# Quarter sums of a Strassen-style transformer block taken on VectorE from PSUM, first keys from eight products, and earlier reloads

## The chip, the core and the metric

The kernel runs on one core of a Trainium2 chip. Five engines work side by side, each with its own in-order instruction stream: TensorE (PE: matmuls, and transposes as matmuls against an identity; PEld is its weight load), VectorE (DVE), ScalarE (ACT), GpSimd (POOL) and SyncE (SP, which here only issues DMAs). They meet through semaphores. SBUF is the working memory, PSUM the memory into which PE writes. The metric is the device time of one execution in microseconds (us). Lower is better.

## The reference

A cross-attention block with an MLP, all in float32: 8 sequences of 256 tokens, width 512, 16 heads of 32, 256 context tokens for each sequence, an MLP of width 2048.

```python
x = layer_norm(hidden_states, ln1_w, ln1_b)
q = x @ q_w + q_b
k = encoder_hidden_states @ k_w + k_b
v = encoder_hidden_states @ v_w + v_b
attn = softmax(where(mask, q k^T / sqrt(32), min))      # per head
hidden = (attn @ v) @ cproj_w + cproj_b + hidden_states
y = layer_norm(hidden, ln2_w, ln2_b)
return hidden + gelu(y @ fc_w + fc_b) @ proj_w + proj_b
```

## The kernel before

**Groups and units.** The 8 sequences are worked as 4 groups of two (512 tokens). Each group has 8 units, one for each of 4 head groups (4 heads, 128 features) and each of the two sequences. `units` lists them; the loop at line 748 walks them. In the turn of unit n, PE makes the scores of unit n+2 (`scores`, L458), DVE takes them from PSUM with the mask and the running minimum (`softmax`, L476), ACT takes the exponential (L486), GpSimd multiplies by the reciprocal sums (`divide`, L500), PE turns the probabilities of unit n (`turn_probs`, L513, evicted in turn by DVE L516 and ACT L518), and PE multiplies them with the values (`attend`, L529; DVE L536 adds the value bias into the attention tile).

**Seven products in place of eight.** Each projection (keys `kT`, queries `qT`, values `v`, output `po`) is cut into quarters, "11", "12", "21", "22", and done by a Strassen scheme of Winograd's form with 7 products of four matmuls (`strassen`, pieces p0 to p6). It needs sums of quarters beforehand: `A_SUMS` of a weight (s2, s3, s4 and a changed "21"), `B_SUMS` of the token operand (t1, t2, t4 and a changed "12"). Each is one `tensor_tensor` of 128x512 by `sum_up`, L167, on the engine named in the call. For token operands, `sums_at` gives the first two to DVE and the last two to GpSimd; the value and output weights are summed on GpSimd, those of keys and queries on DVE. A piece's result leaves PSUM by `made`: on ACT (L374, L393), on DVE with an earlier sum added (L378, L395), or, for the output projection, on GpSimd and DVE together (L437, L438), into a residual tile.

**Through DRAM.** Finished quarters of keys, queries and values are staged in SBUF, stored to DRAM by `store_quarter`, and reloaded by head group (`load_qk`, `load_v`), two buffers to each. All of these go through SP's one queue in program order, as do loads of context (`load_ctx`), tokens (`load_x`), residual (`load_res`), weights, and stores of the hidden state. The eight bias and scale vectors are loaded on GpSimd's queue (L119).

**The order is written out by hand.** Nothing is scheduled by a planner (`manual_schedule`). Two tables say what is slipped into a unit's turn: `between[g, u, i]` (PE pieces, two places) and `aside[g, u, i]` (other work, four places, 3 being the unit's end). `share` deals projection pieces over units by the counts in `ns`; `begin` and `spread` put other work at a place (group, unit, position). While group g attends, group g+1's keys, queries and values are projected, and from group 1 on also an output projection of an earlier group. Group 3 has no next group: it carries the output projections of groups 1 and 2, the MLP's norm of group 0 and the sums of the fc weights. Everything before the loop (from line 694) is the prologue: group 0's three projections and the first two units' softmax.

**PSUM.** Four score banks, two projection banks (`ps_m`), and two banks under the tag `pt`, which turned contexts, turned tokens, turned probabilities and attention results share.

**Attention operand.** `Att` wraps the attention tile of a group with three sum tiles, made by `begin_out`; `sums_at(..., att_in, ...)` sums it later. Group 1's attention is spilled to DRAM and reloaded (`spill_att`, `reload_att`).

**MLP.** From line 807: four groups, each with four rounds of fc (7 products, L848 to L863 the evictions: u1 on ACT; u2, u3, h22, h12, h21 on DVE) and a projection. In group 0, `sum_pw` sums the projection weights on DVE (L805) in each round, and two rounds also sum the fourth block of fc weights; blocks 0 to 2 are summed in group 3 of the attention.

Of the kernel before, what the change touches and what calls it, by code (L numbers as in the profile page):

```python
# [22 lines left out]
def tile_xattn_block(  # L23
# [94 lines left out]
    for vec, n in vecs:  # L118
        nc.gpsimd.dma_start(rows[at : at + n, :], vec.rearrange("(n p) -> n p", p=P))  # L119
        col_of.append(at)  # L120
        at += n
# [121 lines left out]
    with ExitStack() as att:  # L243
# [6 lines left out]
        mbias, ctxT, xnT, vs, qk, probs, stats, att_of, res = ({} for _ in range(9))  # L250
# [17 lines left out]
        def turn_ctx(g):  # L268
            def piece(c):
                if c == 0:  # L270
                    ctxT[g] = tokens_operand(both, "cT", f"ctxT_{g}")
                ps = turned(f"pct_{g}_{c}")
                turn(ps, ctxs[g], c)
                nc.scalar.copy(chunk(ctxT[g], c), halves(ps))

            return [lambda c=c: piece(c) for c in range(NC)]
# [88 lines left out]
        def project_qk(g, tag):  # L365
            w, base = ("k", c_kb) if tag == "kT" else ("q", c_qb)

            def made(n, bank, u):
                o, k = int(n[0]) - 1, int(n[1]) - 1
                st = staged(g, tag, n)  # L370
                for i in range(2):
                    b = col(base, 2 * o + i)
                    if u is None:
                        nc.scalar.activation(  # L374
                            st[:, i, :], bank[:, i, :], AF.Identity, bias=b, scale=1.0
                        )
                    else:
                        nc.vector.scalar_tensor_tensor(  # L378
                            st[:, i, :], bank[:, i, :], b, u[:, i, :], ALU.add, ALU.add
                        )  # L380
                store_quarter(g, tag, o, k, st)

            return strassen(
                f"p{tag}_{g}", lambda: ws[w], lambda: (ctxT if tag == "kT" else xnT)[g], False, made
            )
# [27 lines left out]
        class Att:  # L413


            def __init__(self, g):
                self.t = att_of[g]
                self.sums = work.tile([P, 3, HC, S], F32, tag="as", bufs=1, name=f"as_{g}")
# [102 lines left out]
        def attend(n):  # L521

            g, hg, b = units[n]
            if hg == 0 and b == 0:
                att_of[g] = work.tile([P, NHG, G], F32, tag="att", name=f"att_{g}")
            av = ps_t.tile([P, S], F32, tag="pt", name=f"av_{n}")
            for kc in range(NK):
# [8 lines left out]
            nc.vector.tensor_scalar_add(  # L536
                att_of[g][:, hg, ts(b, S)], av, col(c_vb, hg)
            )
# [33 lines left out]
        def begin_out(g):  # L572
            att_in[g] = Att(g)

        def spill_att(g):
            nc.sync.dma_start(att_dram, att_of[g])
# [14 lines left out]
        def sums_at(place_v, place_g, of_, g, which):  # L591

            begin(*place_v, lambda: sum_up(V, of_[g], B_SUMS, *which[:2]))
            begin(*place_g, lambda: sum_up(GP, of_[g], B_SUMS, *which[2:]))
# [14 lines left out]
        for g in range(NG - 1):  # L609

            work_of = [project_qk(g + 1, "kT"), project_qk(g + 1, "qT"), project_v(g + 1)]
            ns = (1, 2), (1, 2), (1, 1), (1, 2), (1, 2), (1, 2), (1, 1), (1, 1)
            if g == 1:
                work_of.insert(2, project_out(0))
                ns = (2, 2), (1, 2), (1, 2), (2, 2), (2, 2), (1, 2), (2, 2), (1, 2)
# [4 lines left out]
            if g + 2 < NG:  # L620
                between[g, 7, 1] += turn_ctx(g + 2)
                sums_at((g, 7, 3), (g, 7, 3), ctxT, g + 2, ALL)
                begin(g, 1, 3, load_ctx, g + 2)
                begin(g, 3, 3, load_x, g + 2)
                norm_over(
                    g, xs, g + 2, "a", [(5, 1), (5, 2), (6, 1), (6, 2), (6, 3), (7, 1), (7, 1), (7, 2), (7, 2)]
                )
            sums_at((g, 1, 2), (g, 1, 3), xnT, g + 1, ALL)
            begin(g, 0, 3, load_mask, g + 1)
            begin(g, 5, 1, make_mask, g + 1)  # L630
            begin(g, 0, 3, load_qk, g, 2)
            begin(g, 2, 3, load_qk, g, 3)
            begin(g, 5, 3, load_qk, g + 1, 0)
            begin(g, 6, 3, load_qk, g + 1, 1)
            for hg in range(1, NHG):
                begin(g, 2 * hg - 2, 3, load_v, g, hg)
            begin(g, 7, 3, load_v, g + 1, 0)
        g = 1
        begin(g, 0, 0, begin_out, 0)
        sums_at((g, 0, 1), (g, 0, 1), att_in, 0, ALL)  # L640
        begin(g, 0, 3, load_res, 0)
        bias_at(0, g, [(1, 1), (1, 2), (2, 1), (2, 2)])
# [3 lines left out]
        sums_at((g, 7, 1), (g, 7, 1), att_in, 1, ALL)  # L646
        begin(g, 6, 3, load_res, 1)
        bias_at(1, g, [(7, 2), (7, 2), (7, 3), (7, 3)])
        g = NG - 1
        begin(g, 0, 3, load_qk, g, 2)  # L650
        begin(g, 2, 3, load_qk, g, 3)
        for hg in range(1, NHG):
            begin(g, 2 * hg - 2, 3, load_v, g, hg)
        share(g, project_out(1), [(0, 0, 1), (0, 1, 2), (1, 0, 1), (1, 1, 1), (2, 0, 1), (2, 1, 1)])
        share(g, project_out(2), [(3, 0, 1), (3, 1, 1), (4, 0, 1), (4, 1, 1), (5, 0, 1), (5, 1, 1), (6, 0, 1)])
        begin(g, 2, 3, begin_out, 2)
        sums_at((g, 2, 3), (g, 2, 3), att_in, 2, ALL)
# [4 lines left out]
        begin(g, 6, 3, begin_out, 3)  # L662
        begin(g, 7, 1, lambda: sum_up(V, att_in[3], B_SUMS, 0))
# [18 lines left out]
        for q in range(3):  # L682
            begin(g, 0, 3, load_fc, q)
        spread(
            g,
            [(u, i) for u in range(2, 8) for i in (1, 2)],
            [lambda q=q, i=i: sum_fc(q, i) for q in range(3) for i in range(4)],
        )
# [4 lines left out]

        load_ctx(0)
# [4 lines left out]
        load_mask(0)  # L699
# [3 lines left out]
        run(turn_ctx(0))  # L703
        ps = turned("ps_cols")
        nc.tensor.transpose(ps[:, :n_rows], rows, ident[:n_rows, :n_rows])
        nc.vector.tensor_copy(cols, ps[:, :n_rows])
        load_ctx(1)
        ws["c"] = weight("cw", cproj_w)
        sum_up(V, ctxT[0], B_SUMS, 0, 1)
        sum_up(GP, ctxT[0], B_SUMS, 2, 3)  # L710
        sum_up(V, ws["k"], A_SUMS, 0, 1, 2, 3)
        seen, roots, normalise = layer_norm(xs[0], "a0")
        run([*seen, roots, *normalise])
        k, q, v, tx = project_qk(0, "kT"), project_qk(0, "qT"), project_v(0), turn_x(0)
        run(k[:4])
        run(tx)
        load_x(1)
        sum_up(V, xnT[0], B_SUMS, 0, 1)
        sum_up(GP, xnT[0], B_SUMS, 2, 3)
        sum_up(V, ws["q"], A_SUMS, 0, 1, 2, 3)  # L720
        run(k[4:])
        make_mask(0)
        run(q)
        sum_up(GP, ws["v"], A_SUMS, 0, 1, 2, 3)
        load_qk(0, 0)
        run(v[:2])
# [3 lines left out]
        run(v[2:4])  # L730
        divide(0)
        seen, roots, normalise = layer_norm(xs[1], "a1")
        run([*seen[:2]])
        load_qk(0, 1)
        run(v[4:5])
# [3 lines left out]
        run(v[5:])  # L739
        divide(1)  # L740
        run([*seen[2:], roots, *normalise])
        load_v(0, 0)
        run(turn_ctx(1))
        sum_up(V, ctxT[1], B_SUMS, 0, 1)
        sum_up(GP, ctxT[1], B_SUMS, 2, 3)
        sum_up(GP, ws["c"], A_SUMS, 0, 1, 2, 3)
# [27 lines left out]
        sum_up(V, att_in[3], B_SUMS, 1, 2, 3)  # L774
        sum_up(GP, ys[0], B_SUMS, 0, 1, 2, 3)
        run(o)
# [3 lines left out]
    with ExitStack() as mlp:  # L780
# [26 lines left out]
        for g in range(NG):  # L807
# [21 lines left out]
            for q in range(HF // 2):  # L829
# [16 lines left out]

                fc(bank[1], "11", "11", q, True, False)
                nc.scalar.copy(u1, bank[1])  # L848
# [11 lines left out]
                nc.vector.tensor_tensor(h["12"][q], bank[7], u2, ALU.add)  # L860
                gelu("12", 1, h["12"][q])
# [6 lines left out]
                if g == 0:  # L868
                    sum_pw(q)
                    if q < 2:  # L870
                        sum_fc(3, 2 * q, 2 * q + 1)
# [121 lines left out]
```

## Time and profile before

| what | us |
|---|---|
| median of 3 runs (846.02 to 850.85) | 846.16 |
| the profiled execution | 843.05 |
| its span, first to last instruction | 841.3 |
| first scores on PE (L458) | 61.16 |
| first matmul of the MLP (L796) | 440.96 |
| last attend of group 0, 1, 2, 3 (start) | 165.96, 263.85, 342.18, 423.36 |
| busy on POOL in quarter sums (L167, eight rows of groups) | 47.4 |

The mean granted clock of TensorE is 0.970. The two halves read differently: up to 440 us the loop of units and projections, after it the MLP. A busy share is an average over both, so the times of single stretches say more. A wait in the profile is named by the engine that stood, its line, and what released it. Durations of a group of instructions are means unless a single start time is given.

### The profile page before, as it was taken

How to read it: one execution, taken by the hardware profiler on the slowest of the kernel's cores; microseconds unless marked ns; L12 is line 12 of the kernel's file. 1: busy time of each engine (PE TensorE's matmuls, PEld its weight loads, DVE VectorE, ACT ScalarE, POOL GpSimd, SP SyncE). 2: the span in 40 equal slices, each digit the busy share in tenths (PEclk: the TensorE clock that was granted, in tenths of full speed). 3: DMA queues.
4: the chain of work that ended last, by engine and by line, in shares of the span. 5: the costliest groups of instructions: out<-in, count | busy, mean ns of one | idle time of the engine just before them, and what ended most of it. 6: DMA issues, size and time to landing. Idle time of an engine off the chain costs nothing.

```text
span 841.3 us, 12003 instructions
## 1 busy us (share of the span) xinstructions
PE 768.5 (91%) x4417; PEld 636.9 (76%) x4417; DVE 420.1 (50%) x1035; ACT 270.7 (32%) x794; POOL 359.7 (43%) x311
## 2 busy tenths in 40 slices
PE   5687898899969998987689999999999999999997
PEld 4575776677757776865468888888888888888886
DVE  4636576676647675787564764222541234322100
ACT  2114664566436655644302310032101330023100
POOL 5504564277515543966572553132440425213430
PEclk9899899999979999998999999999999999999999
DMA  9422253234222423861129100120004000020001
GB/s 297 169 88 88 67 157 108 76 111 145 88 76 89 152 80 103 264 199 48 52 73 314 63 1 1 51 100 2 1 1 149 2 1 1 25 76 1 1 1 50
DMA packets 56554, 70.79 MB, mean 84 GB/s; under 512 B 3844, under 2 KB 37680, under 8 KB 56368
## 3 DMA queue, kind: packets, MB, share of 16 engines
q1 hardware_dynamic: 55824, 69.22, 24.9%
q0 software_dynamic: 672, 0.81, 0.6%
q8 instruction: 35, 0.57, 0.3%
q14 instruction: 23, 0.19, 0.1%
HBM read 47.99 MB, written 22.02 MB: 83 GB/s over the span
## 4 chain that ended last, share of the span: by engine, by line
PE 74%; DVE 8%; POOL 7%; DMA 5%; issue 3%; ACT 2%; SPq 1%; DVEq 0%; POOLq 0%
PE py L796 23%; PE pf L796 20%; PE ppt L513 6%; PE pqT L310 6%; PE pkT L310 5%; PE pv L310 4%; POOL pr L500 4%; PE s L458 4%; PE av L529 3%; PE po L310 2%; DMA qT<-qT_dram 2%; DMA pw<-in_L_xattn_proj_w_dram 1%; ACT pr L486 1%; DVE fcw L167 1%; DVE pr L476 1%
## 5 line engine op out<-in xcount | busy, mean ns | idle before, releaser
L500 POOL TENSOR_TENSOR pr<-pr,rsum 128x512 f32<-128x512 f32 x128 | 131.4, 1059 | 167.6 <-DVE rsum L498 132.3
L796 PE MATMUL pf<-y,fcw 128*128 128x256 f32 x896 | 195.5, 380 | 1.4 <-DVE u L852 1.4
L796 PEld LDWEIGHTS pf<-y,fcw 128*128 128x128 f32 x896 | 170.9, 191 | 25.7 <-DVE u L852 2.2
L486 ACT ACTIVATE pr<-pr,nmax 128x256 f32<-128x256 f32 x256 | 127.9, 501 | 145.5 <-DVE nmax L476 145.5
L476 DVE CUSTOM_DVE_ANT_0 pr<-s,mb 128x256 f32<-128x256 f32 x256 | 96.1, 416 | 27.8 <-PE s L458 22.3
L866 POOL TENSOR_TENSOR hs<-h,h 128x512 f32<-128x512 f32 x16 | 24.4, 1528 | 187.6 <-PE pf L796 127.4
L796 PE MATMUL py<-pw,h 128*128 128x256 f32 x384 | 84.8, 379 | 0.0
L513 PE MATMUL ppt<-ident,pr 128*128 128x128 f32 x512 | 75.3, 290 | 10.0 <-DVE pt L516 6.0
L796 PE MATMUL py<-pw_t,h 128*128 128x256 f32 x384 | 83.5, 379 | 0.0
L513 PEld LDWEIGHTS ppt<-ident,pr 128*128 128x128 f32 x512 | 60.6, 148 | 29.6 <-issue 15.7
L796 PEld LDWEIGHTS py<-pw_t,h 128*128 128x128 f32 x384 | 72.7, 190 | 9.8
L796 PEld LDWEIGHTS py<-pw,h 128*128 128x128 f32 x384 | 72.7, 190 | 9.8
L310 PE MATMUL pkT<-ctxT,kw 128*128 128x256 f32 x224 | 60.3, 426 | 9.1 <-DVE st_kT L378 5.6
L458 PE MATMUL s<-kT,qT 32*128 32x256 f32 x512 | 43.5, 442 | 21.3 <-DMA qT<-qT_dram 17.4
L310 PEld LDWEIGHTS pkT<-ctxT,kw 128*128 128x128 f32 x224 | 46.8, 216 | 17.7 <-DVE st_kT L378 6.0
L848 ACT COPY u<-pf 128x512 f32<-128x512 f32 x16 | 9.4, 586 | 151.6 <-PE pf L796 149.8
L458 PEld LDWEIGHTS s<-kT,qT 32*128 32x128 f32 x512 | 27.1, 202 | 36.4 <-DMA kT<-kT_dram 16.2
L310 PE MATMUL pv<-vw,ctxT 128*128 128x256 f32 x224 | 53.2, 387 | 1.4 <-ACT st_v L393 1.4
L839 ACT ACTIVATE h<-h,cols 128x256 f32<-128x256 f32 x96 | 43.3, 501 | 25.8 <-DVE h L863 12.7
L310 PE MATMUL pqT<-xnT,qw 128*128 128x256 f32 x224 | 51.3, 382 | 0.0
L486 ACT ACTIVATION_READ_ACCUMULATOR pr<-pr,nmax 128x1 f32 x256 | 48.2, 188 | 0.0
L310 PEld LDWEIGHTS pv<-vw,ctxT 128*128 128x128 f32 x224 | 42.3, 196 | 7.6 <-ACT st_v L393 1.8
(117 smaller groups left out, 962.2 us busy)
## 6 DMA issues: line engine op xcount, KB each, us to landing
ctx<-in_ctx_dram SPq DMA_DIRECT2D x16, 256.0 KB, 4.1
x<-in_x_dram SPq DMA_DIRECT2D x16, 256.0 KB, 3.7
kT_dram<-st_kT SPq DMA_DIRECT2D x16, 256.0 KB, 2.4
qT_dram<-st_qT SPq DMA_DIRECT2D x16, 256.0 KB, 2.2
kT<-kT_dram SPq DMA_DIRECT2D x16, 256.0 KB, 3.1
qT<-qT_dram SPq DMA_DIRECT2D x16, 256.0 KB, 3.6
v_dram<-st_v SPq DMA_DIRECT2D x16, 256.0 KB, 2.2
v<-v_dram SPq DMA_DIRECT2D x16, 256.0 KB, 3.9
```

The costliest lines, as they stand in the source:

```text
L167: eng.tensor_tensor(x[to], x[a], x[b], op)
L310: nc.tensor.matmul(bank[n][:, i, :], l[:, c, ts(i, P)], r[:, c, :], start=first and i == 0 and c == 0, stop=last and c == HC - 1, skip_gro ...
L458: nc.tensor.matmul(banks[j][:, i, :], qT[j * HD : (j + 1) * HD, b * S + i * P : b * S + (i + 1) * P], kT[j * HD : (j + 1) * HD, b * SK : ( ...
L476: nc.vector.tensor_tensor_reduce(pr[:, j, i, :], banks[j][:, i, :], mbias[g][1][:, b, :], scale=-SCALE, scalar=FLT_MAX, op0=ALU.add, op1=A ...
L486: nc.scalar.activation(pr[:, j, i, :], pr[:, j, i, :], AF.Exp, bias=nmax[:, j, i : i + 1], scale=-1.0, accum_out=sums[:, j, i : i + 1],)
L500: nc.gpsimd.tensor_tensor(pr[:, j], pr[:, j], rsum[:, j, :, None].to_broadcast([P, NQ, SK]), ALU.mult,)
L513: nc.tensor.transpose(ps[:, kc, ts(i, P)], probs[n][:, j, i, ts(kc, P)], ident)
L529: nc.tensor.matmul(av[j * HD : (j + 1) * HD, :], vs[g, hg][:, b * NK + kc, ts(j, HD)], pts[n, j][:, kc, :], start=(kc == 0), stop=(kc == N ...
L796: nc.tensor.matmul(ps, lhsT, rhs, start=first, stop=last, skip_group_check=True)
L839: nc.scalar.activation(h[n][q][:, i, :], src[:, i, :], AF.Gelu_apprx_tanh, bias=col(c_fcb, half * HF + 2 * q + i), scale=1.0,)
L848: nc.scalar.copy(u1, bank[1])
L866: nc.gpsimd.tensor_tensor(h["s3"][q], h["11"][q], h["21"][q], ALU.subtract)
```

## The change

**Prologue.** Vector loads go from GpSimd's queue to ACT's, and the mask loads to the front of GpSimd's. Group 0's keys are four quarters of eight matmuls each (`eight`), which need no sums; the first half of group 0's keys and queries (head groups 0 and 1) is written straight into the operand of the scores (`direct`), with no store or reload. The sums of the key weights come after the keys, for group 1. The rest is dealt anew.

**Sums.** `turn_ctx` takes each sum of context quarters per chunk (128x256), with the chunk in PSUM as one input, on DVE; chunks go in the order 0, 2, 1, 3. `attend` does the same for groups 0, 2 and 3 in each head group's second unit. Tokens, reloaded attention, and value and output weights are summed on DVE from SBUF. GpSimd takes none. The sum tiles of `Att` get two buffers.

**Places.** The turned context of group g+2 is split over unit 7 and the next group's unit 0. Pieces are dealt by new counts. Reloads of keys and queries for the next group stand at the end of units 4 and 5 (before: 5 and 6), the third head group's at the end of unit 7, the fourth's at the end of unit 1. In group 3 only fc block 0 is summed; blocks 1 to 3 are summed in the MLP's first three rounds. The sums of the MLP's first operand go from GpSimd to DVE.

```diff
-        nc.gpsimd.dma_start(rows[at : at + n, :], vec.rearrange("(n p) -> n p", p=P))
+        nc.scalar.dma_start(rows[at : at + n, :], vec.rearrange("(n p) -> n p", p=P))
...
                 ps = turned(f"pct_{g}_{c}")
                 turn(ps, ctxs[g], c)
-                nc.scalar.copy(chunk(ctxT[g], c), halves(ps))
-            return [lambda c=c: piece(c) for c in range(NC)]
+                first, second = ps[:, :S], ps[:, S:]
+                nc.scalar.copy(chunk(x, c), halves(ps))
+                if c < HC:
+                    sums = ((second, x["t1"], x["11"]),)
+                else:
+                    sums = (second, x["t2"], x["t1"]), (first, x["t4"], x["t2"])
+                    if g:
+                        sums += ((second, x["12"], x["12"]),)
+                for a, to, b in sums:
+                    nc.vector.tensor_tensor(to[:, h, :], a, b[:, h, :], ALU.subtract)
+            return [lambda c=c: piece(c) for c in (0, 2, 1, 3)]
...
+                direct = g == 0 and o == 0
+                st = None if direct else staged(g, tag, n)
...
+                    to = qk[g, i, tag][:, ts(k, S)] if direct else st[:, i, :]
...
+                if not direct:
+                    store_quarter(g, tag, o, k, st)
...
+            if g == 0:
+                for i in range(2):
+                    qk[g, i, tag] = work.tile([P, G], F32, tag=tag, name=f"{tag}_{g}_{i}")
+            if g == 0 and tag == "kT":
+                return [lambda n=n: eight(f"p{tag}_{g}", n, ws[w], src(), made) for n in QUARTERS]
+            return strassen(f"p{tag}_{g}", lambda: ws[w], src, False, made)
+        def eight(name, n, w, x, made):
+            bank = ps_m.tile([P, 2, S], F32, tag=f"m{turns[0]}", name=f"{name}_{n}")
+            turns[0] ^= 1
+            for i in range(2):
+                for c in range(NC):
+                    nc.tensor.matmul(
+                        bank[:, i, :],
+                        w[f"{n[0]}{c // HC + 1}"][:, c % HC, ts(i, P)],
+                        x[f"{c // HC + 1}{n[1]}"][:, c % HC, :],
+                        start=i == 0 and c == 0,
+                        stop=c == NC - 1,
+                        skip_group_check=True,
+                    )
+            made(n, bank, None)
...
+            x, h, bias = att_in[g], hg % HC, col(c_vb, hg)
+            nc.vector.tensor_scalar_add(x.t[:, hg, ts(b, S)], av, bias)
+            if b == 0 or g == 1:
+                return
+            for to, a in (("t1", "11"),) if hg < HC else (("t2", "t1"), ("12", "12")):
+                nc.vector.scalar_tensor_tensor(
+                    x[to][:, h, :], av, bias, x[a][:, h, :], ALU.add, ALU.subtract
+                )
+            if hg >= HC:
+                nc.vector.tensor_tensor(
+                    x["t4"][:, h, :], x["21"][:, h, :], x["t2"][:, h, :], ALU.subtract
+                )
...
-            ns = (1, 2), (1, 2), (1, 1), (1, 2), (1, 2), (1, 2), (1, 1), (1, 1)
+            ns = (
+                ((1, 2), (1, 2), (1, 1), (1, 2), (1, 2), (1, 2), (1, 2), (1, 0)),
+                ((0, 2), (2, 2), (2, 2), (2, 2), (2, 1), (2, 2), (2, 2), (2, 1)),
+                ((0, 1), (1, 2), (1, 2), (1, 3), (1, 2), (1, 2), (1, 1), (1, 1)),
+            )[g]
...
-                between[g, 7, 1] += turn_ctx(g + 2)
-                sums_at((g, 7, 3), (g, 7, 3), ctxT, g + 2, ALL)
+                tt = turn_ctx(g + 2)
+                if g == 0:
+                    between[g, 7, 0] += tt[:1]
+                    between[g, 7, 1] += tt[1:2]
+                else:
+                    between[g, 7, 1] += tt[:2]
+                between[g + 1, 0, 0] += tt[2:3]
+                between[g + 1, 0, 1] += tt[3:]
...
-            sums_at((g, 1, 2), (g, 1, 3), xnT, g + 1, ALL)
+            sums_at(xnT, g + 1, [(g, 1, 2), (g, 1, 2), (g, 2, 1), (g, 2, 1)])
...
-            begin(g, 0, 3, load_qk, g, 2)
-            begin(g, 2, 3, load_qk, g, 3)
-            begin(g, 5, 3, load_qk, g + 1, 0)
-            begin(g, 6, 3, load_qk, g + 1, 1)
+            begin(g, 4, 3, load_qk, g + 1, 0)
+            begin(g, 5, 3, load_qk, g + 1, 1)
+            begin(g, 7, 3, load_v, g + 1, 0)
+            begin(g, 7, 3, load_qk, g + 1, 2)
+        for g in range(NG):
+            begin(g, 1, 3, load_qk, g, 3)
             for hg in range(1, NHG):
                 begin(g, 2 * hg - 2, 3, load_v, g, hg)
-            begin(g, 7, 3, load_v, g + 1, 0)
+        spread(0, [(u, 1) for u in range(4)], [lambda i=i: sum_up(V, ws["c"], A_SUMS, i) for i in ALL])
...
-        sums_at((g, 7, 1), (g, 7, 1), att_in, 1, ALL)
-        begin(g, 6, 3, load_res, 1)
-        bias_at(1, g, [(7, 2), (7, 2), (7, 3), (7, 3)])
+        sums_at(att_in, 1, [(g, 6, 1), (g, 6, 2), (g, 7, 1), (g, 7, 2)])
+        begin(g, 5, 3, load_res, 1)
+        bias_at(1, g, [(6, 2), (6, 3), (7, 2), (7, 3)])
...
-            [(u, i) for u in range(2, 8) for i in (1, 2)],
-            [lambda q=q, i=i: sum_fc(q, i) for q in range(3) for i in range(4)],
-        )
+        spread(g, [(5, 1), (5, 2), (6, 1), (6, 2)], [lambda i=i: sum_fc(0, i) for i in range(4)])
...
+        run([k[0], *seen, roots, k[1], *normalise])
+        make_mask(0)
+        sum_up(V, ws["q"], A_SUMS, *ALL)
+        run([k[2], *tx])
         load_x(1)
         sum_up(V, xnT[0], B_SUMS, 0, 1)
-        sum_up(GP, xnT[0], B_SUMS, 2, 3)
-        sum_up(V, ws["q"], A_SUMS, 0, 1, 2, 3)
-        run(k[4:])
-        make_mask(0)
-        run(q)
-        sum_up(GP, ws["v"], A_SUMS, 0, 1, 2, 3)
-        load_qk(0, 0)
-        run(v[:2])
+        run(k[3:])
+        sum_up(V, xnT[0], B_SUMS, 2, 3)
+        seen, roots, normalise = layer_norm(xs[1], "a1")
+        for i in range(4):
+            run(q[i : i + 1])
+            sum_up(V, ws["v"], A_SUMS, i)
+        for i in range(3):
+            run([q[4 + i], seen[i]])
+        run([v[0], seen[3], roots])
+        sum_up(V, ctxT[0], B_SUMS, 2)
         scores(0)
         for j in range(HPG):
             softmax(0, j)
-        run(v[2:4])
+        make = [lambda i=i: sum_up(V, ws["k"], A_SUMS, i) for i in range(4)]
+        run([v[1], *normalise[:2], v[2]])
         divide(0)
-        seen, roots, normalise = layer_norm(xs[1], "a1")
-        run([*seen[:2]])
-        load_qk(0, 1)
-        run(v[4:5])
+        run([v[3], *normalise[2:]])
         scores(1)
         for j in range(HPG):
             softmax(1, j)
-        run(v[5:])
+        tt = turn_ctx(1)
+        run([v[4], *make[:2], v[5], v[6], tt[0], *make[2:], *tt[1:]])
         divide(1)
-        run([*seen[2:], roots, *normalise])
         load_v(0, 0)
-        run(turn_ctx(1))
-        sum_up(V, ctxT[1], B_SUMS, 0, 1)
-        sum_up(GP, ctxT[1], B_SUMS, 2, 3)
-        sum_up(GP, ws["c"], A_SUMS, 0, 1, 2, 3)
+        load_qk(0, 2)
...
-        sum_up(V, att_in[3], B_SUMS, 1, 2, 3)
-        sum_up(GP, ys[0], B_SUMS, 0, 1, 2, 3)
-        run(o)
+        for i in ALL:
+            sum_up(V, ys[0], B_SUMS, i)
+            run(o[i : i + 1])
+        run(o[4:])
...
+                ahead = g == 0 and q + 1 < HF // 2
                 fc(bank[1], "11", "11", q, True, False)
+                if ahead:
+                    sum_fc(q + 1, 0, 1)
...
+                if ahead:
+                    sum_fc(q + 1, 2, 3)
...
-                    if q < 2:
-                        sum_fc(3, 2 * q, 2 * q + 1)
```

## The prediction

> **What bounds the kernel now.** I read the page's busy rows first, then the waits of PE, then the chain of waits, then the busy time by 10 us stretches.
>
> ```profile
> PE 768.5 (91%) x4417; PEld 636.9 (76%) x4417; DVE 420.1 (50%) x1035; ACT 270.7 (32%) x794; POOL 359.7 (43%) x311
> ...
> PE   5687898899969998987689999999999999999997
> ...
> DVE  4636576676647675787564764222541234322100
> ...
> POOL 5504564277515543966572553132440425213430
> ```
>
> PE is full in the right half (the MLP: 4 groups of 98.5 us) and has holes in the left one. Warm costs from the timeline: eight matmuls of 128x256 take 1.73 us, eight transposes 1.02, the 16 of one score 1.08, the 16 of one attend 1.00. Everything on PE before the MLP is 896 such matmuls (194 us), 656 transposes (84) and 32 scores and attends (66): 344 us. The MLP's first matmul is at 440.96, so some 97 us there are waiting or a cold clock.
>
> ```profile
> PE s L458 <- DMA qT<-qT_dram: 17.4, 4, 6.8
> ...
> PE pkT L310 <- DVE st_kT L378: 5.6, 1, 5.6
> ...
> PE s L458 <- DVE nmax L476: 4.0, 1, 4.0
> ```
> ```profile
> 30.00:40.00 10.00, 4.39 (x18) 3.48 (x18) 8.84 (x9) 0.59 (x1) 9.10 (x6) 0.83 0.34 114
> ...
> 140.00:150.00 10.00, 6.16 (x48) 4.39 (x47) 3.11 (x13) 3.04 (x9) 4.03 (x4) 0.83 0.24 79
> ...
> 230.00:240.00 10.00, 3.19 (x30) 2.06 (x32) 5.08 (x16) 2.57 (x9) 5.32 (x6) 0.73 0.46 157
> ...
> 320.00:330.00 10.00, 5.83 (x47) 4.12 (x46) 2.22 (x8) 1.95 (x7) 4.03 (x4) 0.84 0.61 183
> ```
> ```profile
> 31.23 1.77 DVE qw L167
> 33.03 1.65 DVE qw L167
> 34.70 1.64 DVE qw L167
> ...
> 58.43 2.60 DMA qT<-qT_dram
> ```
>
> The first fence is wait totals (us, times, longest); the second is span, busy PE, PEld, DVE, ACT, POOL, granted clock, DMA; the third is the chain (start, length). The reader should see three things. Scores wait four times for a reload of queries. In 30 to 40 us PE is idle because DVE adds weight quarters beside GpSimd. And each hole pulls the granted clock down, so it costs more than its length.
>
> **Prologue (0 to the loop's first new softmax, now at 83.87).** I lay the new order out engine by engine with rows of the timeline. Context chunks land as now (copies from 7.42). Each chunk's sums follow on DVE; nearest row: a 128x256 add from PSUM, L378, 0.48 us. Six of them leave DVE free at about 11.6. The key quarters take 8 matmuls each: the cold eight at 11.32 took 3.78 us, the next perhaps 2.5, so quarter three ends near 19.5. (32 matmuls instead of 28 are +0.9 us of PE; the cover is the normalisation below.) DVE meanwhile: cols 0.2, statistics 3.2, wait for GpSimd's root 1.5, normalise 1.9, mask 0.4, four query-weight sums at 0.68: 21.6. Turned x needs the normalised rows (18.4) and four ACT evictions of 0.77: 23.5. Queries start at 24.4 (now 42.4). During them DVE carries 2 x 0.69 + 6 x 0.48 of evictions, four value-weight sums 2.8 and three statistics 2.5: some 10 us against PE's 6.0, so DVE sets it and the last quarter is out at 34.4. It goes straight to the score operand: no 2.20 store, no 2.60 reload. The first scores come at 34.5 instead of 61.16. From there DVE has two softmaxes at 2.9, normalise 1.9, five value evictions 3.4, four key-weight sums 2.8, ctx 1's eight sums from PSUM 3.4, and waits: it reaches the third softmax near 56. That is 28 us earlier; I book **-27**. Bounds -32 (DVE waits overlap) and -16 (the loads: 5.2 MB stand ahead of the queries' use, at the 325 GB/s of the second stretch 16 us, so they are not late; but each DVE wait I missed is on the path). The 8 vector loads move from GpSimd's queue to ACT's: by SP's issue (four in 1.81 us) 3.6 us on ACT after its 1.28 table load, done by 6, ahead of its first copy at 7.42; at GpSimd's 0.52 each it is 6.2, still ahead. PE waited 1.1 for the last of these loads before it turned them; that is inside my 11.15 start. GpSimd's mask loads, now first there, are wanted at 18 and gain nothing.
>
> **The three later reloads.** The keys' and queries' reload is issued a unit earlier (end of unit 4, not 5), and the pieces dealt so that 14 are done by then. A store is 2.2 us, a reload 3.6, a unit 9.2: landed. In group 1 the load leaves SP ahead of the stores of the output projection, whose eviction hung on GpSimd (the 6.8 wait). Holes 3.84, 6.81, 4.2, and cold matmuls behind them: at 145 us score 1.50 for 1.15, transposes 1.97 for 1.09, products 2.34 for 1.89, thus 1.7; at 239 2.6; at 326 1.7. Together 20.8. A quarter I leave to what is late next, DVE and the divide: **-16** (bounds -21, -6). What SP is moved past: third head group's reload stands behind value stores at unit 7, used two units on; the fourth is queued at unit 1, used at unit 4. In group 2 the attention of group 1 is summed from unit 6 on, right behind its reload (5.5 us from issue, some 6 us before use): a DVE wait of 0 to 2, inside the bounds.
>
> **Group turns.** The four context turns of 16 PSUM-to-ACT copies are split two and two, GpSimd's quarter sums (2 x 1.45 behind DVE's) go: which takes the 3.8 us in which PE waited for ACT's context copies. But a turned chunk now holds its PSUM buffer for one or three DVE sums (0.5 to 1.4 us), and attends in odd units hold theirs for one or two more. **-2** (-6 to +4).
>
> **DVE in the loops.** Per unit of group 0: softmax 2.9, copies 1.3, attend and reciprocal 0.6, pieces 1.4, norms 0.7; new: ctx 0.4, x 0.35, attention sums 0.44, output weights 0.35: 8.4 of 9.2 us. It fits on average, but DVE runs in order, and behind a sum stand softmax and evictions that PE waits for. The trace says what a sum costs beside GpSimd: 128x512 fcw 0.68 alone, 1.75 together, qw four times 1.64. The Trainium skill, "SBUF — State Buffer", section "Who interferes with whom", says that a DVE instruction with two SBUF inputs and a GpSimd one that reads SBUF exclude each other in full. It speaks against this change: the sums that left GpSimd meet its divides, 4.04 of every 9.2 us. But it frees those with a PSUM input, and so does the trace (L331, one PSUM input: 0.69 throughout). By the 0.68 row the two dozen two-SBUF sums in the loops would cost no more than counted; by the rule 44% of them wait about 1 us, 10 us of DVE time. With the row alone this term is 0 and the whole sum -53; with the rule and all of it on PE's path +10 and -43. The 1.64 row sides with the rule, but PE has cover in part: I take **+5** (0 to +12).
>
> **Group 3 and the seam.** Eight of twelve fc-weight sums leave DVE (8 x 0.68 = 5.4, and one of 1.75 lies in the chain just where scores wait 4.0 for nmax); GpSimd's attention sums (2 x 1.24 in the chain ahead of its root for the MLP's norm) go; DVE gets eight sums of 0.48 back. The divide-then-resx coupling (DVE idle 3.51, 3.51, 4.88 for L437) stays. **-6** (-11, 0). At the seam GpSimd's chain is reload resx 5.11, bias 5.07, y sums 4.97, resx 1.23, projection 2.84: the 4.97 go to DVE, which waits there anyway; **-5** (-7, -2).
>
> **MLP.** Its first group gets twelve fc sums on DVE, instead of four. DVE's room between one round's last eviction and the next round's u3 is about 5.5 us; today sum_pw 4.24 and two sums 3.43 already cost PE waits of 0.38 and 1.05. Two sums now stand ahead of the eviction of h21, so everything behind is 1.4 (alone) to 3.4 later in rounds 1 and 2: **+3** (0, +6).
>
> Sum: -27 -16 -2 +5 -6 -5 +3 = **-48**. The profiled execution took 843.05 us (span 841.3 and 1.75 around it): 795. The median of the runs shown, 846.16, stands 3.1 above it, so the forecast of a median is **798 us**.
>
> **Rivals.**
> *The prologue saves only half.* DVE there is nearly without a gap, 42 us of work in 48; a PSUM buffer or root that comes late each time moves all. For it: today's prologue has DVE waits of 3.91 and 1.48 us for that root. Saving 14: 811.
> *The stalls only change names.* With the reload early, scores wait for DVE or the divide: 223.55 to 239 shows GpSimd resx ending 231.3 and the reciprocal at 234.96, before the data came. Against it: at 320 to 330 DVE is 22% busy. Reloads worth 5, group 3 nothing: 815.
> *DVE becomes the pace, and it is slower.* Place: units of groups 0 and 1. If shared-port waits and in-order waits raise DVE's 8.4 above 9.2, every unit stretches. From +1.6 us in each of 30 units the whole 48 is gone; at 2.2 it would be 864. Against it: the windows of busy loops show DVE at 69 to 82% now, and most new sums read PSUM.
> *The change does not do what it says* where the sums were off the path: then only the prologue's direct keys remain, some 8 us, 838: no change. Against it: qw's sums are in the chain.
>
> **The numbers.** My forecast (785 to 808) 0.48; better still (765 to 785: prologue and reloads at their ends) 0.15; half a prologue 0.15; renamed stalls 0.15; no change 0.03; slower 0.04. Within 1% (838 to 855) is about what a measurement of this kernel cannot tell from none. Range 775 to 820: it leaves out part of the best case and the last two. Faster 0.93, same 0.03, slower 0.04.
>
> **What would show it.** First scores at 33 to 38; no wait of s on qT; third softmax near 56; DVE share up from 50 to about 55%, POOL busy down by 47 us (the L167 POOL rows sum to that); MLP's first matmul near 390 (440.96 less the 51 before it); first MLP round waits of PE on u2 or u3 of 2 to 4 us. Wrong if PE waits on DVE evictions sum beyond 30 us, or queries start after 32.

## The result

| | us |
|---|---|
| changed kernel, median of 4 runs (809.88 to 814.52) | 811.18 |
| kernel before, same comparison | 846.39 |
| ratio, 95% interval | 0.9579 [0.9542, 0.9616] |
| profiled execution's span | 808.7 |

The change makes the kernel 4.2% faster. That lies inside the range that was forecast, 13 us short of its middle. The profile after, in the order in which the one before was read: the page's busy rows (share, instructions, then tenths of 40 slices), and the waits of PE.

```profile
PE 758.7 (94%) x4425; PEld 630.5 (78%) x4425; DVE 435.1 (54%) x1088; ACT 273.0 (34%) x799; POOL 306.7 (38%) x269
...
PE   5998999799998999996898999999999999999997
...
DVE  3596878566775779685759654234342252322111
...
POOL 2023344246533337766324352034422252232340
```
```profile
PE pct L210 <- DMA ctx<-in_ctx_dram: 7.9, 4, 3.3
PE av L568 <- DVE pt L555: 4.9, 2, 2.5
PE ppt L552 <- DVE att L581: 3.7, 3, 1.5
PE ppt L552 <- DVE ctxT L287: 3.5, 3, 1.4
PE pct L210 <- DVE ctxT L287: 3.1, 4, 1.9
...
PE pf L835 <- DVE fcw L167: 2.3, 1, 2.3
PE av L568 <- DVE ctxT L287: 1.9, 1, 1.9
```

No score waits for queries any more; before, that was 17.4 us in four waits. The largest wait is now for the very first loads. The sums taken from PSUM, `ctxT` and `att` in these rows, are new releasers in the list, some 12 us together. GpSimd is busy 53 us less and DVE 15 us more.

Where the time came from is read from the starts of attends (L529 before, L568 after):

| stretch | before | after | change |
|---|---|---|---|
| start to group 0's first attend | 92.69 | 75.86 | -16.8 |
| from there to group 3's first attend | 259.18 | 251.12 | -8.1 |
| from there to group 3's last attend | 71.49 | 64.86 | -6.6 |
| from there to the MLP's first matmul | 17.60 | 14.74 | -2.9 |
| from there to the end | 400.34 | 402.12 | +1.8 |
| span | 841.3 | 808.7 | -32.6 |

### The profile page after: what moved, and what is told of

Same layout as the page of the kernel before. It is cut to its first block, busy times and chain, and to the rows that moved or that the text cites. A ratio compares the mean times of both kernels' runs of the same rounds, so it can differ in the third digit from the quotient of the medians.

```text
span 808.7 us, 12024 instructions
## 1 busy us (share of the span) xinstructions
PE 758.7 (94%) x4425; PEld 630.5 (78%) x4425; DVE 435.1 (54%) x1088; ACT 273.0 (34%) x799; POOL 306.7 (38%) x269
## 4 chain that ended last, share of the span: by engine, by line
PE 78%; DVE 10%; DMA 4%; POOL 2%; ACT 2%; issue 2%; SPq 1%; DVEq 0%; ACTq 0%; POOLq 0%
PE py L835 24%; PE pf L835 20%; PE pqT L323 6%; PE ppt L552 6%; PE pkT L323 5%; PE pv L323 4%; PE po L323 4%; PE s L497 3%; PE av L568 3%; PE pkT L415 2%; DVE pr L515 2%; POOL pr L539 2%; DMA pw<-in_L_xattn_proj_w_dram 1%; DVE fcw L167 1%; DMA ctx<-in_ctx_dram 1%
## 5 line engine op out<-in xcount | busy, mean ns | idle before, releaser
L555 DVE COPY pt<-ppt 128x512 f32<-128x512 f32 x64 | 43.9, 686 | 5.2 <-PE ppt L552 5.1
L323 PEld LDWEIGHTS pqT<-xnT,qw 128*128 128x128 f32 x224 | 41.6, 190 | 5.2
L878 ACT ACTIVATE h<-pf,cols 128x256 f32<-128x256 f32 x32 | 13.4, 471 | 93.1 <-PE pf L835 93.1
L568 PE MATMUL av<-pt,v 128*32 128x256 f32 x512 | 37.0, 391 | 8.3 <-DVE pt L555 4.9
```

Of the source, the lines that this page charges most:

```text
L323: nc.tensor.matmul(bank[n][:, i, :], l[:, c, ts(i, P)], r[:, c, :], start=first and i == 0 and c == 0, stop=last and c == HC - 1, skip_gro ...
L555: nc.vector.tensor_copy(pt, ps)
L568: nc.tensor.matmul(av[j * HD : (j + 1) * HD, :], vs[g, hg][:, b * NK + kc, ts(j, HD)], pts[n, j][:, kc, :], start=(kc == 0), stop=(kc == N ...
L878: nc.scalar.activation(h[n][q][:, i, :], src[:, i, :], AF.Gelu_apprx_tanh, bias=col(c_fcb, half * HF + 2 * q + i), scale=1.0,)
```

## The experiments

Each ratio is to the kernel before, measured with it on one chip. The changed kernel's is 0.9579; a hundredth is 8.4 us. The kernel before took 844.2 to 846.4 us on the different chips, so gains are taken from the ratios; the medians in us can differ from them by some 2 us. Intervals are about 0.004 wide to each side, so a difference of less than some 4 us between two kernels isn't told from none by the times alone. Times inside a kernel are from one trace each.

**1. Reloads back to their old places.**

```diff
-            begin(g, 4, 3, load_qk, g + 1, 0)
-            begin(g, 5, 3, load_qk, g + 1, 1)
+            begin(g, 5, 3, load_qk, g + 1, 0)
+            begin(g, 6, 3, load_qk, g + 1, 1)
...
-            begin(g, 7, 3, load_qk, g + 1, 2)
...
-            begin(g, 1, 3, load_qk, g, 3)
+            if g:
+                begin(g, 0, 3, load_qk, g, 2)
+            begin(g, 2, 3, load_qk, g, 3)
```

> The reloads of keys and queries go back to the ends of units 5, 6, 0 and 2; the rest of the change stays. Theory A (the earlier place alone took the three waits of scores for their operand, some 16 us with their cold matmuls): three waits of 3 to 7 us are back, the time is 12 to 18 us more, about 826. Rival B (a hole there only lets DVE and GpSimd catch up, and the time comes back at the next turn of groups): the waits are back but the time is only 3 to 7 us more, about 816.

Ratio 0.9855 [0.9821, 0.9889], 832.3 us: 23 us more by the ratios (21 by the medians), beyond theory A. Scores wait for queries again in this kernel:

```profile
PE s L497 <- DMA qT<-qT_dram: 13.8, 3, 5.8
```

13.8 us of waiting cost more than 20: a hole is dearer than its length, and nothing is won back at the next turn of groups. From group 0's first attend to group 3's, the trace is 20.3 us longer for the same PE instructions: PE is idle 14.2 us more, and busy 6.1 us more at a lower granted clock. The stretch in this kernel and in the changed one (length, then busy PE, PEld, DVE, ACT and POOL with instruction counts, granted clock, DMA):

```profile
76.59:348.05 271.46, 243.17 (x1793) 190.39 (x1793) 183.60 (x627) 147.63 (x477) 116.64 (x117) 0.94 0.34 109
```
```profile
75.86:326.98 251.12, 237.06 (x1793) 185.62 (x1792) 183.12 (x627) 147.37 (x477) 117.33 (x117) 0.97 0.38 118
```

**2. The early reloads alone, in the kernel before.** The same edit the other way round, on the old kernel with its own dealing of pieces.

> The kernel before with one part of the change alone: reloads of keys and queries at the ends of units 4 and 5, of the third head group at unit 7, of the fourth at unit 1; its own counts of pieces. Theory A (the holes are simply taken away): no wait of scores for queries in the loop, 18 to 24 us less than before, ratio about 0.975. Rival B (without the rest of the change, DVE and GpSimd are late where the holes were): the waits go, but only 6 to 12 us are gained, ratio about 0.99.

Ratio 0.9749 [0.9716, 0.9781], 823.1 us: 21 us less, theory A. One wait of scores for queries, 2.7 us, is left; it is the prologue's. This one part carries some six tenths of the whole gain. It also shows what the rest of the change does in the loop. The next two fences give busy times of the loop by stretches: group 0's units, its turn (from unit 6's attend to the next group's first), group 1's units, its turn, group 2 up to group 3's first attend. Columns are as above. First the old kernel with early reloads, then the changed one:

```profile
94.45:149.44 54.99, 54.11 (x434) 42.55 (x433) 39.41 (x141) 35.42 (x115) 27.77 (x28) 1.00 0.46 136
149.44:174.36 24.92, 22.23 (x161) 17.26 (x161) 17.99 (x59) 13.15 (x42) 13.51 (x13) 0.93 0.20 64
174.36:239.46 65.10, 63.02 (x473) 50.06 (x472) 43.59 (x153) 37.54 (x124) 38.39 (x37) 1.00 0.42 135
239.46:261.34 21.88, 20.79 (x161) 16.23 (x160) 16.93 (x53) 13.29 (x43) 12.49 (x12) 1.00 0.27 85
261.34:333.61 72.27, 71.39 (x569) 56.21 (x568) 51.21 (x186) 47.24 (x156) 41.33 (x41) 1.00 0.47 139
```
```profile
75.86:133.47 57.61, 56.46 (x441) 44.30 (x440) 45.72 (x157) 36.94 (x119) 25.32 (x26) 1.00 0.40 121
133.47:159.38 25.91, 20.27 (x137) 14.77 (x136) 17.29 (x59) 12.93 (x42) 9.32 (x10) 0.80 0.22 72
159.38:226.47 67.09, 66.09 (x490) 53.11 (x489) 45.20 (x154) 36.65 (x120) 33.94 (x33) 1.00 0.40 127
226.47:249.52 23.05, 19.13 (x146) 14.43 (x145) 16.68 (x56) 12.89 (x42) 9.31 (x10) 0.93 0.44 138
249.52:326.98 77.46, 75.12 (x585) 59.01 (x584) 58.24 (x202) 47.97 (x157) 39.44 (x38) 1.00 0.38 119
```

The old loop with early reloads takes 239.2 us, the changed loop 251.1: the other edits cost 12 us there. The counts say where. The changed kernel deals 39 PE instructions fewer into the two turns (283 against 322), and yet the turns are 2.2 us longer; the three stretches between them, where PE is busy 97 to 98.5% of the time, get 40 more and are 9.8 us longer. The difference is five products, four of keys and one of values, of eight records each. At 0.216 us a record (1.73 for eight), 40 are 8.6 us. In the turns PE waits for a chain of other engines: it is idle there for 9.6 us in place of 3.8, and the clock of the first is 0.80 in place of 0.93. So pieces there look nearly free, and they were taken away. This is read from two traces; the counts were not put back by themselves in a run, so it is not shown as a cause.

**3. First keys and queries through DRAM again.**

```diff
-                direct = g == 0 and o == 0
+                direct = False
...
+        load_qk(0, 0)
+        load_qk(0, 1)
         run([v[0], seen[3], roots])
```

> The first two head groups of group 0's keys and queries go through DRAM again (stored, and reloaded right behind the last query store); all else stays. Theory A (the store of 2.2 and the reload of 2.6 to 3 stand in the path from the last query to the first scores, and only one value product of 1.9 covers them): first scores about 4 us later, and so the loop; time about 815. Rival B (PE and DVE fill the gap with value products and statistics they owe anyway): the loop's first attend within 1 us, time about 811.

Ratio 0.9653 [0.9613, 0.9692], 816.2 us: 6 us more, theory A. Group 0's first attend is at 81.35 instead of 75.86, and scores wait 4.6 us once for their queries.

**4. Seven products for the first keys.**

```diff
-                    if g:
+                    if True:
                         sums += ((second, x["12"], x["12"]),)
...
-            if g == 0 and tag == "kT":
+            if False:
...
+        sum_up(V, ws["k"], A_SUMS, *ALL)
+        run([k[0], k[1], *seen, roots, k[2], k[3], *normalise])
```

> Group 0's keys are done by seven products again, still written straight into the scores' operand for head groups 0 and 1; the sums of the key weights stand ahead of them on DVE, and the context's fourth sum is taken with the others. Theory A (the prologue is bound by PE: a quarter of eight products takes 3.46 us warm, two pieces' worth, so eight products cost 1.7 us more of PE than seven): first scores 1 to 2 us earlier or the same, time 809 to 811. Rival B (my prediction's: the sums are what the eight products take off the path, four of 0.7 on DVE and the wait of p1 for them): first scores 3 to 5 us later, time about 815.

Ratio 0.9586 [0.9551, 0.9622], 810.3 us: no difference in time. First scores came at 50.47, 4 us later, as B says, but 2.2 of that is a later start of the keys (15.81 for 13.61), and by the first attend only 1.75 is left of it. Eight products buy nothing that the times can tell.

**5. Vector loads back on GpSimd's queue.**

```diff
-        nc.scalar.dma_start(rows[at : at + n, :], vec.rearrange("(n p) -> n p", p=P))
+        nc.gpsimd.dma_start(rows[at : at + n, :], vec.rearrange("(n p) -> n p", p=P))
```

> Only the eight vector loads go back from ACT's queue to GpSimd's. Theory A (their issue holds up SP's: in the changed kernel SP's first key-weight load is issued at 4.75 us instead of 2.58, the last context tile is turned at 9.3 instead of 6.9, PE's first key matmul is at 13.61 instead of 11.32, and PE is nearly full from there to the first scores): first key matmul near 11.3, first scores near 44, time 2 to 2.5 us less, about 809. Rival B (the later loads are those the queue would have carried anyway, and queries wait for DVE): first scores stay at 46.4, time within 0.5 us of 811.

Ratio 0.9587 [0.9537, 0.9637]: not told from none. In its trace the first key matmul is at 11.79 and the first scores are at 44.92, 1.8 and 1.5 us earlier, as A says. The starts of all twelve experiments back A on the place: with these loads on ACT's queue, nine kernels start their keys at 12.40 to 15.81 us; with them on GpSimd's, three (experiments 2, 5 and 12, of which 12 also turns the vectors later) start at 10.50 to 11.79. A's reason does not follow from this: the edit also puts the mask and bias loads behind the vector loads again (last section).

**6. Sums on GpSimd again, where no PSUM is read.**

```diff
-            sums_at(xnT, g + 1, [(g, 1, 2), (g, 1, 2), (g, 2, 1), (g, 2, 1)])
+            begin(g, 1, 2, lambda g=g: sum_up(V, xnT[g + 1], B_SUMS, 0, 1))
+            begin(g, 1, 3, lambda g=g: sum_up(GP, xnT[g + 1], B_SUMS, 2, 3))
...
+        sum_up(GP, ws["c"], A_SUMS, *ALL)
...
+        sum_up(GP, ws["v"], A_SUMS, *ALL)
...
+        sum_up(GP, ys[0], B_SUMS, *ALL)
```

> All sums that need no PSUM go back to the engines of the kernel before: GpSimd takes the last two of each tokens operand and of the reloaded attention, all four of the value and output weights and of the MLP's first operand. Context and attention sums stay on DVE from PSUM, and places, reloads and keys stay as changed. Theory A (the sums that were moved to DVE from SBUF are worth little in the loops; only the seam's 5 us are on GpSimd's chain): 4 to 7 us more, nearly all after the last attend, about 816. Rival B (sums on GpSimd exclude DVE's two-operand instructions and delay the divides all over): 10 us and more, the prologue and units 1 of each group longer too, about 823.

Ratio 0.9581 [0.9545, 0.9617]: no change. Both theories missed. In its trace even the sums of the MLP's first operand, 5.06 us on GpSimd, cost little: from the last attend to the MLP it takes 15.52 us instead of 14.74. PE waits once there, for what follows GpSimd's sums; in the changed kernel it waits once for DVE, which then has these sums ahead. This kernel, then the changed one:

```profile
405.25 1.99 PE L323 MATMUL po<-cw,att 128*128 128x256 f32 x8 [2.06 <-DVE resx L477]
```
```profile
399.57 1.99 PE L323 MATMUL po<-cw,att 128*128 128x256 f32 x8 [1.28 <-DVE po_u L344]
```

That no sum is left on GpSimd brought nothing that the times can tell.

**7. Attention sums later, from SBUF.**

```diff
-            if b == 0 or g == 1:
-                return
+            return
...
+        sums_at(att_in, 0, [(g, 0, 1), (g, 0, 2), (g, 1, 1), (g, 1, 2)])
...
```

> The sums of the attention quarters leave attend: they are taken by DVE from SBUF, four of 128x512 a group, at the first two units of the next group (the last group's: one at unit 7, three after the loop). Theory A (in attend they hold the PSUM buffer that turned probabilities need, 3.7 us of waits on them, and their place in DVE's order delays the reciprocals): waits of turned probabilities for att go, the turns of groups 0 and 2 are 1 to 2 us shorter each, but the seam to the MLP is 2 to 3 longer; time 809 to 813. Rival B (taken in PSUM they are free, and SBUF sums collide with the divides): 3 to 6 us more, about 815.

Ratio 0.9582 [0.9546, 0.9619]: no change in time, inside theory A's span. In its trace the step from group 0 to 1 is 15.79 us instead of 17.50, and from the last attend to the MLP it takes 16.75 instead of 14.74, as A says. The waits on `att` fall out of PE's eleven largest; those on reciprocals (2.4) and on the output projection's u (2.6) take their place.

**8. Context sums later, from SBUF, all on DVE.**

```diff
-                for a, to, b in sums:
+                for a, to, b in sums if g < 2 else ():
...
+                between[g, 7, 1] += tt
+                begin(g, 7, 3, lambda g=g: sum_up(V, ctxT[g + 2], B_SUMS, *ALL))
```

> From group 2 on the context is turned in four pieces at unit 7 without sums, and DVE sums it from SBUF at that unit's end, as the kernel before did, but none on GpSimd. Theory A (summing from PSUM holds the two shared buffers while DVE waits for ACT's copy and ACT for DVE's softmax; this made the turn from group 0 to 1 17.5 us from attend to attend where 12.5 were before): that step falls to 12 to 13, the time is 4 to 8 us less, about 805. Rival B (the step is long because DVE's work is too much there whatever its order): the step stays at 16 or more, or unit 7 grows by as much, time 809 to 815.

Ratio 0.9678 [0.9642, 0.9715], 817.3 us: 8 us more, where theory A said 4 to 8 less. The step from unit 7 to the next attend is 16.95, and unit 7 is 12.55 where it was 8.4. This trace's timeline of that step (start, length, idle before in brackets):

```profile
149.09 4.97 DVE L167 TENSOR_TENSOR ctxT<-ctxT 128x512 f32<-128x512 f32 x4
149.31 5.65 POOL L539 TENSOR_TENSOR pr<-pr,rsum 128x512 f32<-128x512 f32 x4 [8.66 <-DVE rsum L537]
154.67 0.68 DVE L555 COPY pt<-ppt 128x512 f32<-128x512 f32 x1
155.50 1.94 PE L552 MATMUL ppt<-ident,pr 128*128 128x128 f32 x8 [6.00 <-DVE pt L555]
```

Four sums of 0.68 take 4.97, and the divide beside them 5.65 instead of 4.04. What DVE owes PE stands behind the sums, PE needs the divide's result too, and it idles 6 us. The step and unit 7 are as B said; the time is 2 us beyond B's span.

**9. Context sums exactly as before, two of them on GpSimd.** Experiment 8 with sums 2 and 3 on GpSimd.

> From group 2 on the context is turned in unit 7 and summed from SBUF at its end, two sums on DVE and two on GpSimd, exactly as in the kernel before; all else as changed. Theory A (summing on DVE from SBUF cost 8 us because DVE was the late engine there; half of it on GpSimd relieves DVE): 2 to 5 us more than the changed kernel, about 814. Rival B (turning all four pieces in one unit is what costs, whoever sums): 7 to 9 us more as with all four sums on DVE, about 819.

Ratio 0.9577 [0.9546, 0.9609]: as the changed kernel. Both theories missed, A by less. So sums from PSUM with the turn split over two units are as good as the old way, and better than DVE alone from SBUF.

**10. Normalise steps in the next unit 0.**

```diff
...
+                spread(g + 1, [(0, 1), (0, 1), (0, 2), (0, 2)], [lambda t=t: norm_part("a", 2, t) for t in range(NT)])
```

> One move on top of the change: the four normalise steps of the next tokens go from unit 7 to the following unit 0, in front of the turns that use them in unit 1. In the changed kernel the step from the last attend of group 0 to the first of group 1 takes 17.5 us, and the chain there goes to and fro between DVE (mins, normalise, context sums) and ACT (exponentials, context copies) with PE at a clock of 0.71. Theory A (DVE's order there, not its amount, sets the step): the step falls by 3 to 6, the whole by 3 to 7 us, about 805. Rival B (DVE has too much in units 7 and 0 together): what unit 7 gains unit 0 loses, time within 1.5 us of 811.

Ratio 0.9532 [0.9499, 0.9565], 805.8 us: about 4 us less than the changed kernel, and theory A's sign, though the intervals still overlap. The step is 15.0, not 17.5, and 14.7 in experiment 12, so DVE's order made 2.5 us of it or a little more.

**11. The fc sums before the MLP again.** The dealing of the kernel before is restored.

> The twelve sums of fc blocks 0 to 2 go back to group 3's units, and block 3's into the MLP's first two rounds, as in the kernel before. Theory A (their move took DVE work off group 3's path, and costs less in the MLP): from the last attend of group 2 to the MLP's first matmul 4 to 8 us more than the 90.2 of the changed kernel, the MLP 1 to 2 us less than its 402.1; time 3 to 6 us more, about 815. Rival B (group 3 is set by GpSimd's chain of divides and residual adds, DVE has room there): group 3 the same, time 1 to 2 us less.

Ratio 0.9610 [0.9574, 0.9646]: 2.6 us more, not told from none. In the trace both halves of theory A stand: 94.35 us from the last attend of group 2 to the MLP instead of 90.19, and the MLP 399.9 instead of 402.1.

**12. Combined.** The edits of 5 and 10, with the turn of the vectors put behind the first key quarter.

```diff
+            if n == "11":
+                first_cols()
             made(n, bank, None)
```

> The changed kernel with the normalise steps in the following unit 0, the vector loads back on GpSimd's queue, and the turn of the vectors behind the first key quarter instead of ahead of it. Theory A (the three lie in different stretches and add: 4, 0 to 2, and 1): 4 to 6 us less than the changed kernel, ratio to the kernel before about 0.951. Rival B (the start is set by the context's DMA alone): the ratio of the normalise move by itself, 0.953.

Ratio 0.9498 [0.9454, 0.9543], 801.4 us: 5.0% faster than the kernel before and the best of all. Its keys start at 10.50 and its first attend is at 70.88.

## Why the prediction was right, and where it was off

The sum rested on PE's waits for reloads and on the first scores, and these are where most of the time was won: reloads 21 us (experiments 1 and 2), the first keys and queries written directly 5 to 6 (experiment 3). That the total lies in the range is in part luck: the prologue came out 10 us worse than booked and the rest of the loop 9, the reloads 4 to 5 better. Of the signs that were named, scores no longer wait for queries, DVE is at 54% and GpSimd is busy 53 us less. First scores (46.40 for 33 to 38), the third softmax (68.71 for 56) and the MLP's start (406.58 for 390) are late, and one sign of being wrong came true: queries start at 32.49, "after 32".

**Prologue, forecast -27, measured -16.8 (-15.2 to the third softmax): the mis-sized term.** "The key quarters take 8 matmuls each: the cold eight at 11.32 took 3.78 us", and "PE's 6.0, so DVE sets it". Each float32 matmul in the code stands in the trace as two records. The eight records at 11.32 were one piece, that is four matmuls. A quarter of eight matmuls is 16 records, and seven query pieces are 56. The chain of waits of the changed kernel (start, length):

```profile
2.18 7.09 DMA ctx<-in_ctx_dram
...
13.68 12.61 PE pkT L415 x48
...
29.20 3.46 PE pkT L415 x16
32.66 12.10 PE pqT L323 x56
```

Three quarters take 12.61 and not the 8.4 of the forecast; queries take 12.10 and not 6.0 or 10. PE, not DVE, leads nearly all the way from 13.7 to 44.8, and first scores come at 46.40 instead of 34.5. The other terms counted records and took the cost of a record, which is consistent. Of the 16.8, some 5.5 are the direct keys and queries (experiment 3, to the first attend) and at most 1.75 the eight products (experiment 4); the rest belongs to the new order as a whole, and no run takes it apart.

**Vector and mask loads, forecast 0.** The vectors' issue took 4.8 us on ACT and not 3.6. "GpSimd's mask loads, now first there, are wanted at 18 and gain nothing" left out what they may cost others: they and the two bias loads behind them now move at the same time as the context and the key weights (last section). The traces put the whole at 1 to 2 us; the times can't tell it.

**Reloads, forecast -16 of at most -21: measured -21 alone, and +23 when undone.** "A quarter I leave to what is late next" was wrong: nothing was.

**Group turns -2 and DVE in the loops +5: together +12.** With reloads at about -20 in the traces and the loop at -8.1, the rest cost 12. The prediction put the price on DVE's waits for GpSimd. But experiment 6 takes some twenty sums off DVE and nothing moves, and the sums themselves hardly waited: the 16 of the tokens took 0.684 us on average, the mean of an undisturbed one, since they fell between divides; the four of the output weights took 0.687, and the four of the reloaded attention 0.853. What the sum put at nothing is the dealing, "the pieces dealt so that 14 are done by then": five products left the turns for stretches where PE is full, and most of the 12 goes with them as far as counts show (experiment 2). Splitting the context's turn and summing it from PSUM is not the price: experiment 9 puts both back as they were and takes the same time.

**The rule weighed against it.** That a DVE instruction with two SBUF inputs and a GpSimd one reading SBUF exclude each other is borne out in the main where they do meet. In experiment 8 a sum takes 1.24 us for 0.68 and the divide 5.65 for 4.04; both end within 5.87, where one after the other would take 6.8. In the MLP two sums take 5.68. The rule did not decide, since in the loop they seldom meet.

**Group 3, forecast -6, measured -6.6;** experiment 11 gives 4.3 of it to the fc sums (69.13 us for this stretch in its trace, for 64.86).

**Seam, forecast -5, measured -2.9.** Its step, "the 4.97 go to DVE", was mis-sized: it is worth 0.8 in the traces (experiment 6), because DVE's own sums then stand in front of PE. Experiment 7 gives 2.0 more to the last group's attention sums, which are now taken in attend.

**MLP, forecast +3, measured +1.8,** and with experiment 11's -2.2 the fc sums are its whole price. DVE and then PE in the second round, with GpSimd's residual add of the same moment:

```profile
430.69 5.68 DVE L167 TENSOR_TENSOR fcw<-fcw 128x512 f32<-128x512 f32 x2
436.28 0.68 DVE L907 TENSOR_TENSOR h<-pf,u 128x512 f32<-128x512 f32 x1
```
```profile
430.58 4.51 POOL L916 TENSOR_TENSOR resm<-resm,projb 128x2048 f32<-128x2048 f32 x1 [5.26 <-DMA resm<-hid_dram]
```
```profile
435.79 7.14 PE L835 MATMUL pf<-y,fcw 128*128 128x256 f32 x32 [2.29 <-DVE fcw L167]
```

The first sum, 4.95 of the 5.68, ends 0.55 us after the one long GpSimd instruction that it met; PE then waits 2.29.

**The rivals.** That the stalls only change names is refuted by 1 and 2. DVE as the pace is not seen: it is busy 54% of the span, and at most 79% of a stretch of the loop. The half prologue came nearest in its size, for another cause: PE's own work. The last rival held in one point: on which engine, and from which memory, the quarter sums are taken made no difference that the times can tell (experiments 6, 7 and 9), except where all the context's fell to DVE from SBUF at once (experiment 8).

## What to carry to other kernels

Before costing added matmuls, tie the trace's instruction count to the calls in the code: a piece that shows as x8 may be four calls, and a stretch sized by the wrong one names the wrong engine. A transfer that PE waits for is worth more than its wait, and moving its issue ahead by one unit was worth more than all the rearranged sums. Where PE waits for a chain of other engines, independent work costs less than where PE is full; two traces speak for this here, and no run shows it by itself. When loads are taken out of a queue, those behind them start earlier: ask what they will meet.

## What the hardware showed

The first loads shared the DMA engines. In the changed kernel SP issues its four context loads from 0.73 us on, as in experiment 5, where the vectors are on GpSimd's queue. Yet the last context tile is turned at 9.31 instead of 5.87, and SP's first key-weight load is issued at 4.75 instead of 2.59. The changed kernel:

```profile
4.27 1.28 ACTq L119 DMA_DIRECT2D rows<-in_L_xattn_fc_b_dram  x1
...
4.75 4.20 SPq L148 DMA_DIRECT2D kw<-in_L_xattn_k_w_dram  x4
```

All kernels here agree on it: the ten with the vectors on ACT's queue turn the last context tile at 7.37 to 11.18 us and issue the first key weight at 4.05 to 4.75; the four with them on GpSimd's, at 5.87 to 6.90 and at 2.58 to 2.59. What the queues moved from 4 to 10 us (packets, MB, share of 16 DMA engines), in the changed kernel and then in experiment 5; q1 is SP's queue, q0 GpSimd's, q10 ACT's:

```profile
q1 hardware_dynamic: 575, 0.80, 47.7%
q0 software_dynamic: 221, 0.59, 38.2%
q10 hardware_dynamic: 52, 0.01, 1.0%
```
```profile
q1 hardware_dynamic: 1623, 2.03, 94.9%
q0 software_dynamic: 239, 0.03, 5.0%
```

The vectors themselves are 0.02 MB in all. With them gone from GpSimd's queue, the mask and the two broadcast biases behind them are issued at 1.49 to 3.31 us instead of 5.81 to 8.34, and their 0.59 MB move just when the context and key weights are due. That makes them a likelier cause than ACT's eight issues. No run moves one without the other, and why SP's queue falls from 2.03 to 0.80 MB, more than GpSimd's gains, stays open.
